# Pacing row gathers by TensorE's steps instead of VectorE's in a two-layer graph kernel

## The chip, the cores and the metric

The kernel runs on one core of a Trainium2 chip. The metric is the device time of one execution in microseconds (us); the runs before the change have a median of 2179.51 us. TensorE multiplies matrices, VectorE and ScalarE work on elements, GpSimd (POOL in the profile) issues the gathers of rows, and SyncE (SP) issues the plain transfers.

## What is computed

The graph has 6250 nodes with 256 features each and 106250 edges sorted by destination, 6250 of them loops from a node to itself. Two layers follow each other. Cut to what matters:

```
# layer 0
S    = x[src]
msgs = relu(relu(S @ W_r.T + b_r) @ W_r.T + b_r)      # r: one of two kinds of edge
agg  = segment_sum(msgs, dst)                          # per node
gates = agg @ W_ih.T + b_ih + b_hh                     # 4 x 256 wide, three parts used
c    = sigmoid(i) * tanh(g);  hn = sigmoid(o) * tanh(c)
x    = layernorm(x + (relu(relu(hn @ W1.T + b1) @ W2.T + b2) @ W3.T + b3))

# layer 1, four heads
h     = x @ W
e     = leaky_relu(a_src[src] + a_dst[dst])
alpha = softmax of e over the edges of one dst
y     = segment_sum(h[src] * alpha, dst) + bias + x
x     = layernorm(x + relu(layernorm(y) * gamma + beta))
```

## The kernel before

Messages of the first layer depend on the source node and the kind of edge alone, so they are computed once for each node and kind and stored in device memory (`parts0`). Layer 0 then gathers, for each tile of 128 edges, the 128 message rows of 256 numbers, and TensorE sums them into their destination nodes by a matmul with a one-hot matrix (`sum0`, L2179). Layer 1 does the same with rows of h and logits (`rows1`), which are weighted on VectorE first (`weighted`, L2445) and then summed (`sum1`, L2565).

There are 782 tiles of edges without the loops, in windows of seven (`WT = 7`) and groups of two windows; a group is 128 destination nodes or fewer. A gather is one indirect DMA that POOL issues (`gather`, L1719). Rows land in a ring of ten windows (`G`).

The order of instructions on each engine is written out by hand. Two loops run over the tiles, one for each layer, and one turn of a loop is called a step. In step n of the first loop (L2210 to L2253) the gather of tile n is issued, the sum of the tile that was gathered `LAG = 4` steps earlier is queued on TensorE, and then `run.step()` queues a piece of each chain that is open. The chains of layer 0 are `turn` (L1922), which takes a finished group out of PSUM and transposes it, and `update` (L1985), which takes four groups (a quad) through the gates (L2010, six results of two matmuls each), the small network (L2034, L2041, L2058), the norm, and the product with W (L2096). An update of a quad queues one of its six gates in every second step; towards the end of the layer it queues one in every step. 98 tiles are gathered earlier, beside the computing of the messages.

The second loop (L2618 to L2660) does the same for layer 1. Its first 21 tiles (`EARLY`) were gathered at the end of layer 0, and `complete` (L2280) adds to them rows that were not in memory yet, one tile a step with three matmuls (L2292). The other chains there are `ahead` (L2306), with the small matmuls of L2366, `weights` (L2378), and `finish` (L2456).

The class `Pace` (L1749) holds gathers back. At the end of each step `passes` notes an instruction, and `hold` makes a gather wait for the one that was noted some steps before:

```
def passes(self):
    traced = nc.cur_bb.bb.instructions
    self.passed.append(next(i for i in reversed(traced) if i.engine == ET.DVE))

def hold(self, move, n, ahead):
    if n % EVERY:
        return
    n -= self.first + ahead
    if n < 0:
        return
```

ET.DVE is VectorE. `ahead` is the number of steps; it is `AHEAD0` or `AHEAD1` (both 6) plus a ramp. In the first loop the ramp begins at 56 steps and loses one in two steps. In the second it begins at 42 and loses one in six, and in the last 42 steps it rises to 21. `EVERY` is 4. Apart from this, each gather waits for the landing of the gather eight before it, and for the last reader of its place in the ring.

Of the kernel before, what the change touches and what calls it, by code (L numbers as in the profile page):

```python
# [38 lines left out]
ET = mybir.EngineType  # L39
# [26 lines left out]
WT = 7  # L66
TC = -(-(E - N) // P)
# [12 lines left out]
EARLY = 3 * WT  # L80
# [5 lines left out]
AHEAD_G = range(AHEAD_W // 2)  # L86
LATE = 3
CR = 16 * WT
AHEAD0 = WT - 1
AHEAD1 = WT - 1  # L90
EVERY = 4
NOROW = NP + P // 2 - 1
SORTED = "the fast path runs only where the chip has found the edges sorted"

# [654 lines left out]
def gnn_kernel(  # L749
# [878 lines left out]
    with tc.If(odd_v == 0):  # L1628
        fast(
            tc, x, WihT, bih, bhh, W1T, b1, W2T, b2, W3T, b3, Wg, att_src, att_dst, bias, gamma,  # L1630
            beta, out, parts0, rows1, slots, cuts, kept, iota_f, iota_p, ident, idx0, idx1,
            first, mark, slot, low_i, tail_i, tail_x, idx_e, own_n, srcs, rowsp, bufs, slot_a, mark_a,
        )
# [8 lines left out]
def fast(  # L1642
# [52 lines left out]
    def tiles_of(w):  # L1695

        own = range(WT * w, min(WT * w + WT, TC))
        return own, range(WT * w, min(WT * w + WT + 1, TC))
# [19 lines left out]
    def gather(to_tile, table, idx):  # L1718
        return nc.gpsimd.indirect_dma_start(  # L1719
            out=to_tile,  # L1720
            out_offset=None,
            in_=table,
            in_offset=bass.IndirectOffsetOnAxis(ap=idx, axis=0),
        )
# [24 lines left out]
    class Pace:  # L1749
# [4 lines left out]

        def passes(self):
            traced = nc.cur_bb.bb.instructions
            self.passed.append(next(i for i in reversed(traced) if i.engine == ET.DVE))

        def hold(self, move, n, ahead):
            if n % EVERY:  # L1760
# [4 lines that stand above are left out]
            tc.add_manual_dep(  # L1765
                move.ins,
                self.passed[n].name,
                mybir.DependencyInfo(mybir.DependencyClass.Sync, mybir.DependencyReason.DATA),
                reason="rows come no sooner than they are wanted",
            )  # L1770
# [38 lines left out]
    def ring(pool, shape, dtype, name, n):  # L1809

        of = rings.setdefault((name, id(pool)), [[], 0])
        if len(of[0]) < n:
            of[0].append(pool.tile(shape, dtype, name=f"{name}_{len(of[0])}"))
        of[1] += 1
        return of[0][(of[1] - 1) % n]
# [35 lines left out]
    with (  # L1851
# [297 lines left out]
        def order_of(g):  # L2149


            t0 = 2 * WT * g
            own = range(t0, min(t0 + 2 * WT, TC))
            sooner = [t0] + [t0 + j for j in range(*MID)]
            return sooner + [t for t in own if t not in sooner]
# [53 lines left out]
        pace = Pace(len(soon))  # L2209
        for n in range(len(soon), TC + LAG):  # L2210
            if n < TC:
                g, t = order[n]
# [15 lines left out]
                move = gather(got[t][:, :D], parts0, idx0[:, t : t + 1])  # L2228
                pace.hold(move, n, AHEAD0 + max(0, 8 * WT - (n - len(soon)) // 2))
                if t == order_of(g)[0] and g > len(AHEAD_G):  # L2230
# [9 lines left out]
            if n >= len(soon) + LAG:  # L2240
                g, t = order[n - LAG]
# [18 lines left out]
    with (  # L2260
# [19 lines left out]
        def complete(t):  # L2280

            w, j = t // WT, t % WT
            if j == 0:
                srcb[w] = (srcb[w], ring(ep, [P, LATE, WT * P], F32, "ohS", 1))
                for q in range(LATE):
                    nc.vector.tensor_scalar(
                        srcb[w][1][:, q, :], srcb[w][0], own_n[:, q : q + 1], None, op0=OP.is_equal
                    )

            more = ring(eps, [P, D + 2 * H], F32, "fps1", 2)[:, :HA]  # L2290
            for q in range(LATE):
                nc.tensor.matmul(  # L2292
                    more,
                    srcb[w][1][:, q, j * P : (j + 1) * P],
                    rows_l[:, q, :HA],
                    start=(q == 0),
                    stop=(q == LATE - 1),
                )
            nc.vector.tensor_add(G[w][:, j, :], G[w][:, j, :], more)
# [235 lines left out]
        def sum1():  # L2535

            while late and len(queue) < 8:
                piece = late.pop(0)
                g, w, o, n = piece[:4]
                gw = weighted(*piece)  # L2540
                queue.extend((g, WT * w + j, gw[:, j, :]) for j in range(n))
            if not queue:
                return
            g, t, gw = queue[0]
            if g not in sums and g >= 2 and g - 2 not in read:
                return
            queue.pop(0)
            if g not in sums:
                sums[g] = ring(eps, [P, D + 2 * H], F32, "fps1", 2)
                left[g] = len(tiles_in(g)[1])  # L2550
                u = everyone
                if g % 2 == 0:
                    k3s[g // 2] = ring(fp, [P, 2, 3, D], F32, "k3", 2)
                of = k3s[g // 2].rearrange("p i c f -> p i (c f)")
                if len(pair_of[g]) == 1:
                    nc.sync.dma_start(of[:, g % 2, :], kept[g // 2, :, g % 2, :])
                elif g % 2 == 0:
                    nc.sync.dma_start(of, kept[g // 2])
            begins = left[g] == len(tiles_in(g)[1])
            left[g] -= 1  # L2560
            j = t - 2 * WT * g
            to, cols = place(j, MID[1])
            ohj = ohs[g][:, cols]
            ends = left[g] == 0 or j in (WT - 1, TC - 1 - 2 * WT * g)
            nc.tensor.matmul(sums[g][to, :], ohj, gw, start=begins, stop=ends)  # L2565
            if left[g] == 0:
                run.start(finish(g, sums[g]), 1)
# [48 lines left out]
        pace = Pace(0)  # L2616
        t = 0
        while t < TC + LAG or late or queue or run.chains:  # L2618
            if EARLY <= t < TC:
                w = t // WT  # L2620
                if t % WT == 0:
                    G[w] = ring(rowsp, [P, WT * HA], F32, "G", 10).rearrange(
                        "p (j f) -> p j f", f=HA
                    )
                move = gather(G[w][:, t - WT * w, :], rows1, idx1[:, t : t + 1])
                brought.setdefault(w, []).append(move)
                pace.hold(move, t, AHEAD1 + max(0, 6 * WT - (t - EARLY) // 6, 3 * WT - (TC - t) // 2))
            k = t - LAG
            if 0 <= k < TC:
                if k < EARLY:  # L2630
                    complete(k)
                w = k // WT
                g = w // 2
                pair = pair_of[g]
                box = boxes[pair[0]]
                if k % (2 * WT) == 0:
                    if g == pair[0]:
                        box["e"] = ring(ep, [P, 2 * GS, H], F32, "e", 3)
                    if g:

                        old = pair_of[g - 1]
                        ob = boxes[old[0]]
                        nc.scalar.copy(  # L2643
                            ob["e"][:, old.index(g - 1) * GS + 2 * WT, :], G[w][:, 0, D:HA]
                        )
                        if old is not pair:
                            run.start(weights(old, ob))
                if k == tiles_of(w)[0][-1] and (w % 2 or w == NW - 1):
                    for v in (w, w - 1) if w % 2 else (w,):
                        o = pair.index(g) * GS + WT * (v % 2)  # L2650
                        own = len(tiles_of(v)[0])
                        nc.scalar.copy(box["e"][:, o : o + own, :], G[v][:, :own, D:HA])
                    if w == NW - 1:
                        run.start(weights(pair, box))
            sum1()
            if len(queue) + W8 * len(late) > 3 * W8 or t % 7 == 0 or t >= TC - 4 * WT:
                sum1()
            run.step()
            pace.passes()
            t += 1  # L2660
# [62 lines left out]
```

## Time and profile before

| what | value |
|---|---|
| median of 10 runs | 2179.51 us (2174.97 to 2182.95) |
| profiled execution, its own time | 2174.84 us |
| its span, first to last instruction | 2173.1 us |
| mean granted TensorE clock | 0.834 |
| TensorE busy | 1580.9 us, 73% |
| VectorE busy | 1313.8 us, 60% |
| ScalarE busy | 513.5 us, 24% |
| POOL busy | 1545.4 us, 71% |
| gathers of layer 0 in the first loop | 712, the first at 224.4 us, the last at 1124.1 us |
| gathers of layer 1 in the second loop | 761, the first at 1157.4 us, the last at 2122.7 us |

In a line of a group the columns are the line of the code, engine, operation, output and inputs, count, then busy time in us and the mean ns of one, then the idle time of the engine just before these instructions and what ended most of it. "issue" means that the engine waited for nothing that the profile shows. PE is TensorE, DVE VectorE, ACT ScalarE. In an answer on waits the columns are who waited for whom, us in total, times, and the longest. In the chain of waits and in the timeline a line begins with the start and the duration in us. Each float32 matmul of the code leaves two records.

### The profile page before, as it was taken

Reading aid. Unit: us, or ns where it says so; the run is one execution under the profiler, and the core shown is the slowest. Engines: PE = TensorE matmul, PEld = TensorE weight load, DVE = VectorE, ACT = ScalarE, POOL = GpSimd, SP = SyncE. Lnnn points to the kernel's source line nnn. Section 1 sums busy time; section 2 is a strip of 40 time slices with the busy share of each in tenths; the row PEclk is TensorE's granted clock in tenths of the full one; section 3 lists DMA queues with packets and bytes.
Section 4 is the critical chain, followed back from the end, with each engine's and each line's share of the span. In section 5 each row is a group of like instructions: output and inputs, shape, how many; then the busy total and the mean of one; then the engine's idle time right before and its main releaser. Section 6 shows DMA issues by size and latency. Waiting matters only on the chain.

```text
span 2173.1 us, 22000 instructions
## 1 busy us (share of the span) xinstructions
PE 1580.9 (73%) x6127; PEld 845.0 (39%) x6127; DVE 1313.8 (60%) x3629; ACT 513.5 (24%) x1656; POOL 1545.4 (71%) x1610
## 2 busy tenths in 40 slices
PE   8988899888888888899977556556465555555563
PEld 5656544333333343344545333333233333333332
DVE  8854345434333433434444788888777777778786
ACT  3333033112221221122341122222222222221222
POOL 2466677777777777777776777777777777777770
PEclk9999999899988999899997777677676767676776
DMA  5356546445554555445555565565555555555551
GB/s 159 113 174 189 176 130 212 150 137 169 168 167 128 159 170 166 144 143 172 185 156 162 158 166 149 151 166 148 154 148 152 149 151 149 152 151 150 151 152 40
DMA packets 153969, 335.05 MB, mean 154 GB/s; under 512 B 37114, under 2 KB 74848, under 8 KB 153837
## 3 DMA queue, kind: packets, MB, share of 16 engines
q0 software_dynamic: 76048, 208.01, 34.7%
q1 hardware_dynamic: 75613, 122.50, 17.5%
q10 hardware_dynamic: 2176, 3.05, 0.4%
q8 instruction: 50, 0.82, 0.2%
q14 instruction: 82, 0.67, 0.1%
HBM read 280.91 MB, written 52.52 MB: 153 GB/s over the span
## 4 chain that ended last, share of the span: by engine, by line
PE 31%; DVE 29%; DMA 12%; issue 8%; POOL 8%; ACT 5%; SPq 0%; ACTq 0%; DVEq 0%; POOLq 0%
PE fps L2179 10%; DVE gw L2445 8%; POOL G L1719 8%; PE fpg L2010 7%; DMA G<-parts,fidx 7%; PE fps L2565 4%; DVE oh L1836 4%; DMA G<-rows,fidx 3%; PE fpg L2096 1%; DVE fst L2495 1%; DVE ohT L2352 1%; PE fps L2292 1%; ACT fy L2503 1%; PE fpm L1573 1%; DVE fy L2480 1%
## 5 line engine op out<-in xcount | busy, mean ns | idle before, releaser
L1719 POOL DMA_INDIRECT G<-rows,fidx x761 | 734.7, 965 | 231.8 <-issue 189.8
L1719 POOL DMA_INDIRECT G<-parts,fidx x712 | 680.5, 956 | 230.1 <-issue 185.8
L2565 PE MATMUL fps<-gw,oh 128*64 128x264 f32 (+1 forms) x1674 | 466.2, 468 | 183.2 <-DVE gw L2445 183.2
L2179 PE MATMUL fps<-G,oh 128*64 128x257 f32 (+1 forms) x1674 | 500.8, 421 | 111.5 <-DMA G<-parts,fidx 103.7
L2565 PEld LDWEIGHTS fps<-gw,oh 128*64 128x64 f32 (+1 forms) x1674 | 240.3, 176 | 329.2 <-DVE gw L2445 198.1
L2179 PEld LDWEIGHTS fps<-G,oh 128*64 128x64 f32 (+1 forms) x1674 | 211.4, 157 | 374.4 <-DMA G<-parts,fidx 163.2
L2445 DVE TENSOR_TENSOR gw<-G,bank 128x1792 f32<-128x1792 f32 (+1 forms) x167 | 248.9, 1490 | 57.9 <-ACT gw L2444 55.4
L2010 PE MATMUL fpg<-faT,fWihT 128*128 128x512 f32 (+2 forms) x432 | 170.0, 517 | 0.2 <-DVE faT L1946 0.2
L1836 DVE TENSOR_TENSOR oh<-bank,fslot 128x448 f32<-128x448 f32 (+2 forms) x315 | 155.1, 547 | 11.9 <-ACT bank L2424 7.4
L1928 DVE TENSOR_SCALAR kind<-fps 128x1 f32<-128x1 f32 x112 | 12.4, 152 | 211.0 <-PE fps L2179 211.0
L1573 PE MATMUL fpm<-fWrT,fhT 128*128 128x256 f32 x392 | 95.0, 394 | 14.2 <-DVE fms L1581 14.2
L1607 POOL DMA_INDIRECT G<-parts,fidx x70 | 70.4, 1005 | 39.3 <-issue 19.4
L2010 PEld LDWEIGHTS fpg<-faT,fWihT 128*128 128x128 f32 x432 | 71.1, 190 | 66.9 <-issue 57.2
L2497 ACT ACTIVATE frs<-fmv,eps_c 128x1 f32<-128x1 f32 x112 | 32.9, 294 | 269.9 <-DVE fmv L2496 133.1
L2130 DVE COPY nd<-hr 128x4 f32<-128x4 f32 x53 | 9.8, 185 | 140.2 <-ACT hr L2102 140.2
L1559 PE MATMUL fph<-fxc,fWrT 128*128 128x512 f32 (+1 forms) x208 | 89.6, 581 | 4.4 <-DMA fWrT<-in_WrT_dram 4.3
L2393 PE MATMUL turn<-fident,e 128*120 128x128 f32 (+2 forms) x30 | 12.3, 412 | 109.3 <-ACT e L2643 109.3
L1573 PEld LDWEIGHTS fpm<-fWrT,fhT 128*128 128x128 f32 x392 | 75.3, 196 | 32.3 <-DVE fms L1581 12.4
L2503 ACT ACTIVATE fy<-fy,frs 128x256 f32<-128x256 f32 x112 | 66.8, 597 | 87.4 <-DVE frs L2500 87.2
L2366 PE MATMUL pn<-node,ohT 128*128 128x24 bf16 (+1 forms) x560 | 35.7, 192 | 69.2 <-DVE ohT L2352 65.6
L2096 PE MATMUL fpg<-Wx,fyT 128*128 128x264 f32 x224 | 71.5, 446 | 3.0 <-ACT fyT L2087 3.0
L2366 PEld LDWEIGHTS <-ohT 128*128 128x128 bf16 x560 | 28.5, 107 | 110.8 <-DVE ohT L2352 76.6
(351 smaller groups left out, 1987.5 us busy)
## 6 DMA issues: line engine op xcount, KB each, us to landing
kept<-keep SPq DMA_DIRECT2D x26, 768.0 KB
k<-kept SPq DMA_DIRECT2D x26, 768.0 KB
loop<-parts SPq DMA_DIRECT2D x55, 256.0 KB
parts<-fms SPq DMA_DIRECT2D x49, 256.0 KB
G<-parts,fidx POOLq DMA_INDIRECT x782
G<-rows,fidx POOLq DMA_INDIRECT x761
dB<-slots SPq DMA_DIRECT2D x26, 320.0 KB
out_dram<-fy SPq DMA_DIRECT2D x56, 128.0 KB
```

The source lines that it names most:

```text
L1559: nc.tensor.matmul(ph[:, :cols], WrT_s[:, r, k, m * P : (m + 1) * P], xc[:, k, :cols], start=(k == 0), stop=(k == 1),)
L1573: made = nc.tensor.matmul(pm[:, r, :], hT[:, r, k, j * P : (j + 1) * P], WrT_s[:, r, k, :], start=(k == 0), stop=(k == 1),)
L1607: nc.gpsimd.indirect_dma_start(out=of[:, n % WT, :D], out_offset=None, in_=parts0[: 2 * P * block, :], in_offset=bass.IndirectOffsetOnAxis ...
L1719: return nc.gpsimd.indirect_dma_start(out=to_tile, out_offset=None, in_=table, in_offset=bass.IndirectOffsetOnAxis(ap=idx, axis=0),)
L1836: nc.vector.tensor_tensor(to[:, o : o + len(js) * n].rearrange("p (j s) -> p j s", s=n), iota_s[:, None, cols].to_broadcast([P, len(js), n ...
L2010: nc.tensor.matmul(pg[:, :cols], WihT_s[:, k, c * P : (c + 1) * P], aT[:, k, :cols], start=(k == 0), stop=(k == 1),)
L2096: nc.tensor.matmul(ph[u, :], hs[i][:, k, u], Wx[:, k, :], start=(k == 0), stop=(k == 1))
L2179: nc.tensor.matmul(sums[g][to, :], ohj, got[t], start=begins, stop=ends)
L2366: nc.tensor.matmul(to, ohT[:, j, :], of_n, start=True, stop=True)
L2445: made = nc.vector.tensor_mul(gw[:, :, :D].rearrange("p j (h f) -> p j h f", h=H), of[:, :n, :D].rearrange("p j (h f) -> p j h f", h=H), e ...
L2503: nc.scalar.activation(y, y, AF.Identity, bias=m, scale=r)
L2565: nc.tensor.matmul(sums[g][to, :], ohj, gw, start=begins, stop=ends)
```

## The change

The notes are taken of TensorE (ET.PE) instead of VectorE, each second gather is held instead of each fourth, and by two steps instead of six; the ramp of the first loop and that of the last 42 steps stay, and the ramp at the start of the second loop goes.

```diff
-AHEAD0 = WT - 1
-AHEAD1 = WT - 1
-EVERY = 4
+AHEAD0 = 2
+AHEAD1 = 2
+EVERY = 2
...
-            self.passed.append(next(i for i in reversed(traced) if i.engine == ET.DVE))
+            self.passed.append(next(i for i in reversed(traced) if i.engine == ET.PE))
...
-                pace.hold(move, t, AHEAD1 + max(0, 6 * WT - (t - EARLY) // 6, 3 * WT - (TC - t) // 2))
+                pace.hold(move, t, AHEAD1 + max(0, 3 * WT - (TC - t) // 2))
```

## The prediction

> **What bounds the kernel now.** I read the page first (engine shares, groups by line), then who waited for whom on POOL, then the timeline and the chain of waits around one update, then TensorE's timeline where the second layer begins. From the page:
>
> ```profile
> L1719 POOL DMA_INDIRECT G<-rows,fidx x761 | 734.7, 965 | 231.8 <-issue 189.8
> L1719 POOL DMA_INDIRECT G<-parts,fidx x712 | 680.5, 956 | 230.1 <-issue 185.8
> ```
>
> The idle time before these gathers is nearly all "issue", that is, no wait. The waits of POOL between 300 and 1000 us say it plainly:
>
> ```profile
> POOL G L1719 <- issue: 147.7, 485, 0.3
> POOL G L1719 <- DMA G<-parts,fidx: 5.8, 19, 0.3
> POOL G L1719 <- DVE agg L1932: 2.8, 9, 0.3
> ```
>
> No entry is longer than 0.3 us, also where a releaser is named. A gather costs about 0.95 busy plus 0.30 between two, and starts every 1.25 us, mostly without a break: in the first layer from 224.36 to 1124.14 us, in the second from 1157.39 to 2122.66 us (965 us for 760 periods, 1.27 each). The last gather starts 50 us before the end of the span. So the gathers' issue sets the time. The waits of before cost nothing, hence their removal brings nothing; what a new wait takes from POOL is never caught up, because POOL has no spare time.
>
> **What the change removes.** Two kinds of pacing wait on VectorE: 182 plus 169 gathers named VectorE's semaphore in the built program, 30 in the changed one. Value zero, by the 0.3 us above. The order of instructions on every engine stays as it was. Also removed is the head start of the second layer (six windows, 42 steps, shrinking by one in six): until now the gathers of the second layer could run far ahead of the loop.
>
> **What it adds.** 683 of some 1,500 gathers now wait for TensorE's semaphore (149 before), and POOL gets 191 more semaphore instructions. Of those 17 ns is the usual duration and they run on POOL's sequencer while the gathers ahead are still being issued; I cost them at zero (at most 191 x 17 ns = 3 us without that cover). Behind a held gather all later gathers are queued on POOL, and behind those TensorE's sums (first layer) and ScalarE's copies of logits (second). TensorE's last instruction of step n-2 comes after the sum of tile n-6, as the sums lag the gathers by four. Gather n-6 started 6 x 1.25 = 7.5 us earlier, a landing takes 2.7 to 6.0 us (pieces of the chain), the sum's four records with the next about 1.0. So where TensorE only follows the gathers, the wait costs nothing; it costs where TensorE falls behind them.
>
> **Term 1, the first layer's updates.** The chain of waits between 560 and 600 us runs through one of them:
>
> ```profile
> 571.96 1.72 PE fpg L2010 x4
> 573.68 1.01 PE fps L2179 x4
> 574.69 1.91 PE fpg L2010 x4
> 576.60 1.01 PE fps L2179 x4
> 577.61 1.91 PE fpg L2010 x4
> 579.53 0.93 PE fps L2179 x4
> 580.46 1.91 PE fpg L2010 x4
> 582.37 1.01 PE fps L2179 x4
> 583.39 1.91 PE fpg L2010 x4
> 585.30 1.01 PE fps L2179 x4
> 586.31 1.91 PE fpg L2010 x4
> 588.23 1.01 PE fps L2179 x4
> ```
>
> While the six gates of a quad (L2010) go by, TensorE takes 2.92 us for two steps (a gate and two sums); two gathers take 2.50. The gates end at 573.68, 576.60, 579.53, 582.37, 585.30 and 588.23. The gathers that will wait for them now start, by POOL's timeline, at 573.63, 576.13, 578.63, 581.13, 583.63 and 586.13. The first is just late, the last by 2.10; with a release of 0.27 (below) the hold is 2.4 us in this update. Afterwards TensorE catches up and waits for gathers again (84 us in 131 waits between 300 and 1000 us), so the next update costs anew. The old ramp, which stays, covers the updates before 365 us (112 gathers at 1.25). Nine updates with this pattern follow, at 367 to 940 us: 9 x 6 x 0.42 = 23. The one at 996 us has a gate in each step: 2.49 us a step against 1.25. Its six gates are three pairs, 3 x 2.48 = 7.4, less what the first pair has in hand, 7. The two short ones up to 1075 us: 3.28 us a pair for a few pairs, 3. Together 33. Laying each gather beside its instruction in the whole stage gives 94 of 324 that would be late.
>
> The price of a release is read where POOL already waits for TensorE:
>
> ```profile
> 213.57 10.52 PE fps L2179 x36
> 224.10 0.26 issue
> 224.36 0.94 POOL G L1719
> ```
>
> TensorE ends at 224.09, the gather starts 0.27 later; the one at 242.80 shows the same. Bounds for a release: nothing (if the sequencer hides it) and a whole period of 1.25. I take 0.27, the row of the same wait. By the bounds the term goes from 29 to about 55: each update then also loses up to 1 us at its first hold, and as much margin, two pairs more.
>
> **Term 2, the start of the second layer.** With the head start gone, the gather of tile 22 (the second of the loop, 1158.64 us) waits for step 20. TensorE's timeline there:
>
> ```profile
> 1160.47 12.42 PE L2292 MATMUL fps<-rows_l,ohS 128*128 128x260 f32 x42 [8.84 <-DMA srcb<-srcs]
> ...
> 1189.20 1.56 PE L2292 MATMUL fps<-rows_l,ohS 128*128 128x260 f32 x6
> 1190.60 0.25 PE L2366 MATMUL pn<-node,ohT 128*128 128x24 bf16 x4
> ```
>
> Tile 16 is completed in step 20 (L2292, six records a tile; the rows up to 1189.20 make 102, seventeen tiles), and after it come the four matmuls that end at 1190.85. 1190.85 + 0.27 - 1158.64 = 32.5 us, in which POOL now issues 26 gathers and will issue none. From then on TensorE gains on POOL: held against their steps, the gathers of before are late by 32 us at 1159, by 19 at 1201, by 10 at 1366, early by 2 at 1432, and never late after 1500. So it is one hold, not many, and since POOL then runs at 1.27 us to the last gather, it is paid in full. Both sides: nothing, if the end were set by VectorE (78% busy from 1500 us) and the head start were idle; against that ScalarE waits for the pair's last gather 33 times, 91.8 us. Above: 40, if the half clock (granted 0.50 from 1139.2 to 1166.5 us) lasts longer into these steps. I take 32.5.
>
> **Sum.** 33 + 32.5 = 66. The profiled execution took 2174.84 (span 2173.1): 2241. Its median of runs is 4.7 higher, 2179.51, so I state 2245. By the bounds: 2179.5 + 29 + 32 = 2241 and 2179.5 + 55 + 40 = 2275, wider where terms fail.
>
> A rule that speaks against a cheap hold: TensorE: Matmul & The Clock Gate, Part 1, says that TensorE's clock halves after an idle window of about 3.4 us. The trace has the row for what that costs: four matmuls of L2096 take 2.13 us at 1140.27, where the granted clock is 0.50, and 1.16 at 1122.64, where it is 1.00, and the mean granted clock was 0.92 from 300 to 1000 us. A hold falls where TensorE is busiest and the time lost comes back as some 3 us of waiting an update, in pieces, so I take no further half clock. By the rule, if each of twelve updates brought one such window, an estimate of 12 x 1.7 = 20 us more, 2265.
>
> **Rivals.** (1) Only the start of the layer costs: the update's lateness is made up between two gates, for POOL's sequencer already waits several us ahead of the issue. Then 2179.5 + 32.5 = 2212. Against it: 2.92 against 2.50 holds in every pair, and nothing gives POOL the time back. (2) The second layer holds too: TensorE waits there for VectorE's weighted rows (149.5 us in 45 waits from 1300 to 2100, up to 7.6), and the smallest lead of a gather over its step after 1500 us is 0.1 us. With 2 us for each of 27 pairs of groups: 66 + 54, 2300. Against it: nine in ten of the leads after 1500 are over 3 us. (3) Faster: with fewer gathers queued ahead, a gather becomes cheaper. The place is the 1.27 us of the second layer, which could fall to the shortest period in the trace, 0.942 + 0.30 = 1.24: 760 x 0.03 = 23 us, giving 2157 if no hold remained. It decides once the holds together cost under 23 us; Term 2 alone is above that. That the change does not do what it says is out, since the 683 waits stand in the built program.
>
> **How the numbers follow.** My forecast 0.68, rival 1 0.14, rival 2 0.14, rival 3 0.04 with half of it no change. The range 2210 to 2285 takes in the forecast with its bounds and clock, and rival 1; it leaves out rivals 2 and 3, 0.18. About 0.2%, 4 us, is what can be told from no change here (the runs spread from 2174.97 to 2182.95). Faster 0.02, same 0.02, slower 0.96.
>
> **What would show it.** Right: POOL's waits name L2010 with about 50 holds of 0.3 to 1 us up to 1110 us and one of over 25 us before the second layer's second gather; the last gather starts some 66 us later, the tail of 50 us is the same. Wrong: no TensorE entry over 0.3 us on POOL in the first layer (rival 1); steady holds by L2565 after 1500 us (rival 2); gathers at less than 1.25 us (rival 3).

## The result and the profile after

The changed kernel takes 2247.0 us (2241.96 to 2254.74) against 2179.12 us of the kernel before in the same comparison: the ratio is 1.0317, 95% interval 1.0306 to 1.0327. Its profiled execution took 2246.43 us, of which its span is 2244.6 us, 71.5 more than before. The mean granted clock is 0.830 (0.834 before).

The page of the kernel after, the two groups of gathers (count, then busy us and mean ns of one, then the idle time before them and what ended most of it):

```profile
L1719 POOL DMA_INDIRECT G<-rows,fidx x761 | 736.4, 968 | 266.6 <-issue 204.7
L1719 POOL DMA_INDIRECT G<-parts,fidx x712 | 679.6, 954 | 265.0 <-issue 165.8
```

A gather costs what it cost within a few ns (968 ns against 965, and 954 against 956; the 3 ns make some 2 us over the second loop). The idle time grew, by 34.8 us in one layer and by 34.9 in the other. Who ended it is in the waits of POOL, whole span (us in total, times, longest):

```profile
POOL G L1719 <- issue: 375.6, 1227, 2.2
POOL G L1719 <- PE fpg L2010: 45.8, 58, 2.8
...
POOL G L1719 <- PE fps L2179: 35.3, 72, 12.3
POOL G L1719 <- PE pn L2366: 35.0, 2, 34.7
```

About 0.30 us of each entry is the usual distance of two gathers, so the totals are read less 0.30 each. L2010 then has 28.3 us in 43 held gathers, and L2366 one hold of 34.4. L2179 is the exception to keep out: 12.3 of its 35.3 is the first gather of the loop, which was held as long before the change (12.4); nearly all its others are the usual 0.30.

One update in POOL's timeline (start, duration, then in brackets the idle time before it and its releaser):

```profile
731.76 0.94 POOL L1719 DMA_INDIRECT G<-parts,fidx  x1 [1.23 <-PE fpg L2010]
733.01 0.94 POOL L1719 DMA_INDIRECT G<-parts,fidx  x1 [0.30 <-issue]
734.69 0.94 POOL L1719 DMA_INDIRECT G<-parts,fidx  x1 [0.73 <-PE fpg L2010]
735.94 0.95 POOL L1719 DMA_INDIRECT G<-parts,fidx  x1 [0.30 <-issue]
737.61 0.94 POOL L1719 DMA_INDIRECT G<-parts,fidx  x1 [0.73 <-PE fpg L2010]
738.86 0.95 POOL L1719 DMA_INDIRECT G<-parts,fidx  x1 [0.30 <-issue]
```

and TensorE in the same update:

```profile
729.61 1.88 PE L2010 MATMUL fpg<-faT,fWihT 128*128 128x512 f32 x4
731.42 1.08 PE L2179 MATMUL fps<-G,oh 128*64 128x257 f32 x4
732.43 1.98 PE L2010 MATMUL fpg<-faT,fWihT 128*128 128x512 f32 x4
734.35 1.08 PE L2179 MATMUL fps<-G,oh 128*64 128x257 f32 x4
735.36 1.98 PE L2010 MATMUL fpg<-faT,fWihT 128*128 128x512 f32 x4
```

The gates end at 731.49, 734.41 and 737.34, and held gathers start at 731.76, 734.69 and 737.61, 0.27 or 0.28 later: each second one waits, and the pair takes 2.92 us, TensorE's two steps, where it took 2.50. TensorE itself waits for nothing between these gates, not for rows either. The start of the second loop, on POOL:

```profile
1192.54 0.95 POOL L1719 DMA_INDIRECT G<-rows,fidx  x1 [0.30 <-issue]
1228.18 0.94 POOL L1719 DMA_INDIRECT G<-rows,fidx  x1 [34.69 <-PE pn L2366]
1229.42 0.94 POOL L1719 DMA_INDIRECT G<-rows,fidx  x1 [0.30 <-issue]
1230.91 0.94 POOL L1719 DMA_INDIRECT G<-rows,fidx  x1 [0.54 <-PE fps L2292]
```

and on TensorE in the same stretch:

```profile
1198.40 11.75 PE L2292 MATMUL fps<-rows_l,ohS 128*128 128x260 f32 x42 [11.63 <-DMA srcb<-srcs]
...
1226.26 1.56 PE L2292 MATMUL fps<-rows_l,ohS 128*128 128x260 f32 x6
1227.65 0.25 PE L2366 MATMUL pn<-node,ohT 128*128 128x24 bf16 x4
```

TensorE's part of step 20 ends at 1227.90, and the gather that waits for it starts 0.28 later. From there on nearly nothing is held. The waits of POOL after 1500 us have no entry longer than 0.3 us:

```profile
POOL G L1719 <- issue: 146.2, 480, 0.3
POOL G L1719 <- DMA G<-rows,fidx: 8.2, 27, 0.3
POOL G L1719 <- PE fps L2565: 6.1, 20, 0.3
```

The account, from the first and last start of the gathers in the two traces:

| stretch | before | after | difference |
|---|---|---|---|
| first gather of the first loop | 224.4 | 226.8 | +2.5 |
| first to last gather, layer 0 | 899.8 | 933.9 | +34.1 |
| last of layer 0 to first of the second loop | 33.3 | 31.8 | -1.5 |
| first to last gather, second loop | 965.3 | 1001.7 | +36.5 |
| last gather to the end of the span | 50.4 | 50.3 | -0.1 |

### The profile page after: what moved, and what is told of

Its sections match the earlier page's. It is cut to its first block, busy times and chain, and to the rows that moved or that the text cites. A ratio compares the mean times of both kernels' runs of the same rounds, so it can differ in the third digit from the quotient of the medians.

```text
span 2244.6 us, 22191 instructions
## 1 busy us (share of the span) xinstructions
PE 1601.2 (71%) x6127; PEld 849.5 (38%) x6127; DVE 1310.4 (58%) x3629; ACT 514.1 (23%) x1656; POOL 1547.8 (69%) x1610
## 4 chain that ended last, share of the span: by engine, by line
PE 25%; POOL 19%; DVE 18%; issue 15%; DMA 13%; ACT 3%; SPq 0%; POOLq 0%; ACTq 0%; DVEq 0%
POOL G L1719 19%; PE fps L2179 9%; DMA G<-rows,fidx 6%; DMA G<-parts,fidx 6%; DVE gw L2445 6%; PE fps L2565 5%; PE fpg L2010 3%; DVE oh L1836 3%; PE fps L2292 1%; PE fpg L2096 1%; PE fpm L1573 1%; DVE ohT L2352 1%; PE fpg L2034 1%; DVE fst L2495 1%; PE fph L1559 1%
## 5 line engine op out<-in xcount | busy, mean ns | idle before, releaser
L2179 PE MATMUL fps<-G,oh 128*64 128x257 f32 (+1 forms) x1674 | 509.9, 422 | 134.4 <-DMA G<-parts,fidx 125.8
L2565 PE MATMUL fps<-gw,oh 128*64 128x264 f32 (+1 forms) x1674 | 473.0, 476 | 184.5 <-DVE gw L2445 184.5
L2565 PEld LDWEIGHTS fps<-gw,oh 128*64 128x64 f32 (+1 forms) x1674 | 243.1, 179 | 334.1 <-DVE gw L2445 200.2
L2179 PEld LDWEIGHTS fps<-G,oh 128*64 128x64 f32 (+1 forms) x1674 | 208.7, 157 | 406.3 <-DMA G<-parts,fidx 191.2
L2010 PE MATMUL fpg<-faT,fWihT 128*128 128x512 f32 (+2 forms) x432 | 170.7, 519 | 0.2 <-DVE faT L1946 0.2
L1928 DVE TENSOR_SCALAR kind<-fps 128x1 f32<-128x1 f32 x112 | 12.4, 152 | 237.8 <-PE fps L2179 237.8
L2010 PEld LDWEIGHTS fpg<-faT,fWihT 128*128 128x128 f32 x432 | 71.7, 191 | 67.7 <-issue 57.7
L2366 PE MATMUL pn<-node,ohT 128*128 128x24 bf16 (+1 forms) x560 | 35.6, 192 | 64.6 <-DVE ohT L2352 58.2
L2366 PEld LDWEIGHTS <-ohT 128*128 128x128 bf16 x560 | 28.5, 107 | 105.9 <-DVE ohT L2352 69.3
```

What stands on the lines that cost most here:

```text
L2010: nc.tensor.matmul(pg[:, :cols], WihT_s[:, k, c * P : (c + 1) * P], aT[:, k, :cols], start=(k == 0), stop=(k == 1),)
L2179: nc.tensor.matmul(sums[g][to, :], ohj, got[t], start=begins, stop=ends)
L2366: nc.tensor.matmul(to, ohT[:, j, :], of_n, start=True, stop=True)
```

## The experiments

The experiments ran on two kinds of chip: on some the kernel before takes about 2180 us, as in the prediction, on others about 2700. Every ratio is to the kernel before on the same chip. The first kind answers the question of this change and comes first; the second is told after it.

The theory is the prediction's: two losses, each paid in full, one from TensorE's slower steps in the updates of the first layer and one from the head start that is gone. In the expectations, A is a rival that charges about 0.1 us for every one of the waits that name TensorE, wherever they stand; B is the rival that a lateness is made up later; C is the rival that TensorE as the noted engine is the cause, and not distance and head start. E is that rows that land late, and not the gates, make TensorE late. S1 and S2 are theories of the slower chips: by S1 gathers that run far ahead slow TensorE, by S2 TensorE's results come late there, and a gather that waits for VectorE waits for the whole chain behind them.

**The change itself, on the chip of the next two kernels.**

> The change itself, beside the kernel before on the same chip. Where the kernel before takes about 2180 us: 66 us over it again. Where it takes about 2700 us, as in the six runs so far: all kernels with TensorE as the noted engine took 2584 to 2593 us there whatever the distance and the head start, so about 2585 us, ratio 0.957. Then the question is what the notes of VectorE cost there. Theory S2: TensorE's results come up to 10 us late on those chips, VectorE stands in front of them, and a gather that waits for VectorE's step six back waits for the whole chain. Theory S1: gathers that run far ahead slow TensorE itself.

2252.36 us against 2180.08, ratio 1.0337 (1.0313 to 1.0361). Layer 0's gathers take 943.7 us from first to last, and the idle time of POOL at the start of the second loop is 32.0, a hold of 31.7 over the usual 0.30. It is the reference for the two below.

**No pacing at all.** The kernel before, in which no gather waits for a noted instruction:

```diff
 def hold(self, move, n, ahead):
-    if n % EVERY:
-        return
+    return
```

> The kernel before without any pacing wait in both loops; a gather waits only for the gather eight before it and for its place in the ring. Where the kernel before takes about 2180 us: the theory says that its pacing waits cost and bring nothing, so within 4 us of it; a rival (early gathers crowd the other transfers) says 10 to 40 us slower. Where it takes about 2700 us: theory S2 says that this is at least as fast as the change, 2585 us or less, since no gather waits for VectorE's chain; theory S1 says that it is the slowest, 2710 us or more, since gathers run furthest ahead.

2178.64 us, ratio 0.9993 (0.9983 to 1.0003). The waits that the change removed were worth nothing in either direction. POOL's waits in that run show what an unheld queue looks like:

```profile
POOL G L1719 <- issue: 423.0, 1389, 0.3
```

Its gathers take 901.6 us in layer 0 and 965.3 in the second loop. The change on the same chip therefore costs 943.7 - 901.6 = 42.1 us in layer 0, more than the 34.1 of the first comparison, and 999.6 - 965.3 = 34.3 us in the second loop.

**The same distances, noted of VectorE.** The change with one word put back:

```diff
-            self.passed.append(next(i for i in reversed(traced) if i.engine == ET.PE))
+            self.passed.append(next(i for i in reversed(traced) if i.engine == ET.DVE))
```

> The change with VectorE as the noted engine: two steps back, each second gather, no head start, but VectorE's last instruction of the step. Where the kernel before takes about 2180 us: the theory (the distance of two steps and the missing head start are the cause, since VectorE's instructions of a step end about when TensorE's do) says 60 to 70 us over it; rival C (TensorE as the noted engine is the cause) says at most 10. Where it takes about 2700 us: S2 says above 2710 us, since the same waits for VectorE come four steps earlier; S1 says about 2585 us, as the gathers are held as closely as in the change.

2252.89 us, ratio 1.0335 (1.0314 to 1.0355), 72.8 us over the kernel before: the same time as the change. The waits of POOL in this kernel name VectorE instead:

```profile
POOL G L1719 <- issue: 349.6, 1128, 3.2
...
POOL G L1719 <- DVE G L2299: 32.3, 1, 32.3
POOL G L1719 <- DVE agg L1932: 23.2, 27, 3.6
...
POOL G L1719 <- DVE fgg L2023: 14.7, 12, 4.8
```

C falls. Layer 0's gathers take 939.6 us here and 943.7 with the change, so where gathers are held, a step of VectorE ends about as late as one of TensorE. What costs is that each second gather is tied to a step two back, and that the head start is gone. Which engine is noted makes no difference here. How the first layer's loss divides between the distance (six steps to two) and the count (each fourth gather to each second) no run on these chips shows.

**The head start alone.** The change with the ramp of the second loop put back:

```diff
-                pace.hold(move, t, AHEAD1 + max(0, 3 * WT - (TC - t) // 2))
+                pace.hold(move, t, AHEAD1 + max(0, 6 * WT - (t - EARLY) // 6, 3 * WT - (TC - t) // 2))
```

> The change with the head start of the second loop back, a third time, hoped for on a chip where the kernel before takes about 2180 us. There: the theory of two separate losses says 33 to 36 us over it (2213 to 2216 us), with POOL's holds of the first layer as in the change, and none over 3 us after 1160 us. Rival A (0.1 us for each wait that names TensorE, 673 of them): 67 us. Rival B (the first layer's lateness is made up in the second): none. Where it takes about 2700 us: ratio 0.957 to 0.960 as twice before.

2221.47 us against 2183.24, ratio 1.0185 (1.0161 to 1.0209): +38.2 us, where the change has +72.3 on the chip of the two kernels above and +67.9 in the first comparison (it was not run on this one). So 30 to 34 us come back with the head start alone. The 38.2 that stay are 2 to 5 more than expected, as layer 0 loses 42 here and not 33. In this kernel the waits of POOL, whole span and then from 1160 to 2200 us:

```profile
POOL G L1719 <- issue: 378.0, 1234, 2.2
POOL G L1719 <- PE fpg L2010: 51.4, 59, 3.4
```

```profile
POOL G L1719 <- issue: 213.0, 699, 0.3
POOL G L1719 <- PE fps L2565: 9.8, 28, 1.5
POOL G L1719 <- DMA G<-rows,fidx: 7.3, 24, 0.3
```

The first layer's holds are as large as with the change (943.8 us from first to last gather, 943.7 there), while no hold in the second loop is longer than 1.5 us, and that loop takes 968.3 us, 3.0 more than unpaced. A falls, since about half the waits of the change lie in the second loop and cost almost nothing there. B falls twice: the first layer's loss stays to the end, and taking away the one hold of the second loop brings back all but 3.0 us of it.

**On the slower chips.** The kernel before takes about 2700 us here.

> The change with one part undone: the head start of the second loop (42 steps, one less in six) is back; TensorE's step two back and each second gather stay in both loops. Theory (two separate losses: 33 us because TensorE takes 2.92 us for two steps of an update where two gathers take 2.50, and 32.5 us because the gather of tile 22 waits for step 20): the second loss goes, the first stays, so 33 to 36 us over before, 2212 to 2215 us, and no hold over 3 us after 1160 us. Rival A (each wait that names TensorE costs POOL about 0.1 us wherever it stands, 68 us over 683 of them): 673 waits remain, so about 67 us over before, 2246 us. Rival B (one loss alone, felt at the end of the second layer, and the first layer's lateness is made up there): no loss, 2180 us.

The head start put back, as above: 2584.34 us against 2702.71, ratio 0.9567 (0.954 to 0.9593).

> The change in the second loop alone; the first loop waits for VectorE, each fourth gather, six steps back, as before. Theory: the first loss goes, the second stays: 32 to 35 us over before, 2211 to 2214 us, with one hold of 32 to 35 us at the second gather of the second loop and none over 1 us elsewhere in it. Rival A (0.1 us a wait): 465 gathers name TensorE, 149 did before, so about 32 us too, but spread over the loop and with no long hold. Rival B (the head start is idle time, TensorE and VectorE set the end of the second layer): 2180 us.

The first loop as before (notes of VectorE, each fourth gather, six back), the second as changed:

```diff
-AHEAD0 = 2
+AHEAD0 = WT - 1
...
-        pace = Pace(len(soon))
+        pace = Pace(len(soon), ET.DVE, 4)
...
-        pace = Pace(0)
+        pace = Pace(0, ET.PE, EVERY)
```

2635.85 us, ratio 0.9772 (0.9734 to 0.981).

> The change with each gather held in place of each second; 1263 gathers name TensorE in place of 683. Theory (the pace of TensorE's steps sets the loss, not the number of waits): the bound is tighter by at most one gather at the beginning of an update, so 68 to 72 us over before, 2247 to 2251 us. Rival A (0.1 us a wait): 1263 waits, about 126 us over before, 2305 us.

Every gather waits (`EVERY = 1`): 2584.07 us, ratio 0.957 (0.9544 to 0.9597).

> The change with six steps back in place of two, in both loops; TensorE, each second gather, and no head start in the second loop stay. 679 gathers name TensorE. Theory: four steps more give 5 us of slack in an update, more than the 2.5 us by which its gates fall behind, so the first loss almost goes (1 to 4 us left); in the second loop the gather of tile 26, five periods later than that of tile 22, waits for step 20, so 32.5 - 5 = 27.5 us are left: 28 to 32 us over before, 2207 to 2211 us. Rival A (0.1 us a wait): 67 us, 2246 us. Rival C (TensorE as the engine that is noted is the cause, at any distance): between 60 and 67 us.

Six steps back instead of two (`AHEAD0 = AHEAD1 = WT - 1`, TensorE, each second gather, no head start): 2593.09 us, ratio 0.9599 (0.9576 to 0.9622).

The times of these four contradict every expectation, the theory's too: there these kernels are 2 to 4% faster than the one before. What could still be read is where the holds stand. With two steps back POOL is held once at the start of the second loop, in the timeline of e2_layer1_only:

```profile
1435.50 0.95 POOL L1719 DMA_INDIRECT G<-rows,fidx  x1 [0.30 <-issue]
1467.96 0.94 POOL L1719 DMA_INDIRECT G<-rows,fidx  x1 [31.51 <-PE pn L2367]
```

With six steps back the gather waits for a step four earlier, and the hold is shorter, in the timeline of e4_six_back:

```profile
1390.36 0.95 POOL L1719 DMA_INDIRECT G<-rows,fidx  x1 [0.30 <-issue]
1415.36 0.95 POOL L1719 DMA_INDIRECT G<-rows,fidx  x1 [24.05 <-PE fps L2292]
1416.61 0.94 POOL L1719 DMA_INDIRECT G<-rows,fidx  x1 [0.31 <-issue]
1420.23 0.95 POOL L1719 DMA_INDIRECT G<-rows,fidx  x1 [2.67 <-PE fps L2292]
```

With six steps the holds sum to 26.6 us over the usual 0.30 each (23.75, 2.37, and 0.51 for a third of 0.81), with two to 31.2. Most of this hold comes from the head start that is gone, then, and not from the six steps that became two. What a hold costs there is another matter: e3_every1 has a hold of 31.5 us too, and takes as long as e1_ramp_back, whose longest in the second loop is 10.0.

Two of these kernels on another chip, which is of the same slower kind:

> The kernel of the first experiment (head start of the second loop back, all else as changed) once more, since there the kernel before itself took 2703 us and TensorE's results came up to 6 us later than their records end. Where the kernel before takes about 2180 us again, the theory of two losses expects 33 to 36 us over it, with no hold over 3 us after 1160 us; rival A (0.1 us for each wait that names TensorE) 67 us; rival B (the first layer's lateness is made up) none. Where the kernel before takes about 2700 us again, the ratio of the first time, 0.957, should come back.

> The kernel with six steps back in place of two (TensorE, each second gather, no head start) once more, for the same reason. Where the kernel before takes about 2180 us: the theory expects 28 to 32 us over it (27.5 at the second loop's start, five periods less than 32.5, and 1 to 4 us in the first layer); rival A 67 us; rival C (TensorE as the noted engine is the cause at any distance) 60 to 67 us. Where it takes about 2700 us: 0.960 again.

2584.01 against 2695.39, ratio 0.9592 (0.9559 to 0.9626), and 2590.06, ratio 0.9588 (0.9551 to 0.9625). Both are as expected after the first chip: the sign there is no accident of one chip.

**Gates spread over three steps**, which should take the late steps of an update away and with them Term 1, on two chips:

```diff
-                    yield (slow + 1) // 2
+                    yield 3 if slow == 3 else (slow + 1) // 2
```

> The change with one more edit: the updates of full quads (but the last) queue one gate in every third step instead of every second. TensorE then takes about 1.91 + 3 x 0.5 = 3.4 us for three steps in which POOL issues three gathers in 3.75, so it no longer falls behind at the gates. Where the kernel before takes about 2180 us: the theory says that 23 of the first layer's 33 to 38 us go, the second loop's 32 to 34 us stay, and the updates near the end of the layer stay: 43 to 52 us over before, about 2228 us, and few holds by L2010 before 990 us. Rival A (0.1 us for each wait that names TensorE) and rival E (late landings, not the gates, make TensorE late): 66 to 72 us over before as in the change. Where it takes about 2700 us: no forecast but 0.95 to 0.97.

> The change with a gate in every third step once more, hoped for on a chip where the kernel before takes about 2180 us. There: the theory says that about 23 of the first layer's 33 to 38 us go, so 43 to 52 us over before, with few holds by L2010 before 990 us and the second loop's hold of 32 to 34 us unchanged; rivals A and E say 66 to 72 us. Where it takes about 2700 us: 0.965 again.

2604.15 against 2696.97, ratio 0.9654 (0.9618 to 0.9691), and 2606.91 against 2722.41, ratio 0.9569 (0.9528 to 0.961), where 0.965 was expected again. Both fell on slower chips, where the change itself was not run, so they say nothing of Term 1. That the pace of the gates makes the first loss rests on the traces of the first kind: the holds name L2010, a held pair takes TensorE's 2.92 us, and TensorE waits for no rows between the gates shown, which speaks against E. It isn't shown by an edit.

## Why the prediction was right

**The bound.** The prediction held that POOL's issue sets the time and that what it loses is never caught up. The account shows it: 34.1 and 36.5 us lost between gathers, and 71.6 at the last gather, with the tail unchanged. Undoing one loss returned that loss alone.

**Removed waits, zero.** The kernel without pacing: 0.9993.

**Term 1, 33 us.** Measured 34.1, and 42.1 on another chip of the same kind. It was counted as 54 holds in full updates of 0.42 each (23 us) with 10 for the late ones; the trace has 43 held entries that name L2010, with a median gap of 0.73, that is 0.43 over the usual: 36 up to 964 us, with 19.4 us, and seven after 1000 us, with 8.9. The first hold of an update was often larger, 0.93 over the usual in the one shown and 2.5 at most; the upper bound allowed up to 1 us for it. Ten more holds, 8.1 us together (one at L1943 of 1.9, others at L2041, L2034, L2083 and L2179, one without a name), had no term in the sum. So the mechanism is the stated one, with fewer and in part larger holds, but that 33 meets 34.1 so closely is partly luck: misses cancel in it, and the same kernel loses 42.1 on another chip. That spread lies inside the bounds of 29 to 55.

**Term 2, 32.5 us.** Measured 34.4 (31.7 on the other chip). The release cost 0.28 against the 0.27 assumed. The remaining two come from TensorE's first matmuls of this stage: they started 5.9 us after the loop's first gather (1198.40 - 1192.54), where before it was 3.1 (1160.47 - 1157.39). The wait ahead of them, for the indices that `srcb` holds, grew from 8.84 to 11.63 us. From those matmuls' start to the end of step 20 it was shorter, 29.5 us against 30.4; the half clock (granted 0.50 up to 1203.1 us) reached 4.7 us into them, where it was 6.0. The term was worked out on the old trace's TensorE, which itself moved a little.

**The clock.** The prediction weighed a rule against the row and took no further half clock. The granted clock from 300 to 1000 us is 0.92 in both traces, so it stayed. The rule named there (the Trainium skill, TensorE: Matmul & The Clock Gate, Part 1, on idle windows of about 3.4 us) allowed an estimate of 20 us more; no run here shows these 20 us.

**The rivals.** Rival 1, lateness made up between gates, needed no entry of TensorE over 0.3 us on POOL in the first layer; there are 43 of L2010 alone, and the loss stays. Rival 2, steady holds in the second layer, needed L2565 over 0.3 us after 1500 us; its longest is 0.3. Rival 3, cheaper gathers, needed periods under 1.25 us; the gathers of the second layer take 968 ns, not less than 965, and start every 1.27 us after the hold, as before.

**What the prediction missed.** The 2.5 us by which the first loop starts later lie ahead of the first held gather. The unpaced kernel, with none of the change's waits, starts it at 226.9 as well and the change itself at 224.8 on that chip, so this looks like a spread of executions and no effect. And it had nothing on chips of the second kind.

## What to carry to other kernels

When one engine issues back to back to the end, a wait added to it costs its full lateness at every place where the waited-for engine runs slower than the issue, and nothing where it runs ahead; so lay each gather beside the instruction it would wait for, stage by stage, and sum only the late ones. A slack of a few steps is used up by the slowest stretch, and a head start at the change of stages can be worth as much as all the rest. Price the distance before the choice of engine: here two steps back cost the same by either. And compare on one chip: all this holds where the kernel before takes about 2180 us, while neighbours of the change gained 2 to 4% on the slower chips.

## What the runs showed of the hardware

The chips on which the kernel before takes about 2700 us were not expected. The kernel before has a mean granted clock of 0.76 to 0.77 there against 0.83 to 0.84; by their ratio, an estimate, that is some 9%, and does not account for 24%. In the records of e1_ramp_back, waits on TensorE can end long after the recorded end of the matmul they wait for. Rows of its timeline:

```profile
727.51 0.44 PE L1943 MATMUL fpg<-fident,agg 128*128 128x128 f32 x2
...
733.84 0.62 PE L2179 MATMUL fps<-G,oh 128*64 128x257 f32 x2 [0.46 <-DMA G<-parts,fidx]
734.72 0.42 DVE L1946 COPY faT<-fpg 128x256 f32<-128x256 f32 x1 [7.57 <-PE fps L2179]
735.04 0.95 POOL L1719 DMA_INDIRECT G<-parts,fidx  x1 [3.19 <-PE fps L2179]
```

The copy of L1946 reads what L1943 left at 727.95 and starts at 734.72, 6.8 us later, while POOL's gather is held 3.19 us. With each of the 56 copies of L1946 laid beside its own two matmuls, six start over 5 us after their end in that run, and this one, 6.8, is the longest; in the six runs on chips of the first kind none starts over 0.84 us after. The transfers are not what is late: the last packet of a gather of layer 0 ends 2.45 us after the issue at the median, 2.44 in the changed kernel's trace.

One caution: the traces of the slower chips hold only part of the semaphores' updates. In e1_ramp_back 1916 are on record for 3228 instructions of VectorE, where h_ramp_back has 3228 for 3228, and 28% of those of the landings. So the lengths of the waits there can be trusted, as they come from starts and ends, but the names of what ended them less.

Why TensorE's results come late there is not known, nor why pacing then helps. In e2_layer1_only, whose first loop waits for VectorE as before, POOL is held by VectorE:

```profile
POOL G L1719 <- issue: 191.6, 616, 3.1
POOL G L1719 <- DVE agg L1933: 45.9, 12, 5.6
POOL G L1719 <- DVE fmv L2064: 33.5, 9, 6.8
POOL G L1719 <- DVE faT L1947: 31.6, 7, 7.9
```

and its layer 0 takes 1097.0 us from first to last gather, against 1055.8 in e1_ramp_back, whose first loop waits for TensorE at two. That would agree with holding being dearer by VectorE, which stands one late result behind TensorE. The kernel before has no trace there, and the change itself, the notes of VectorE at two steps and the unpaced kernel, which would have told S1 from S2, were not run there, so it stays open.
